# Rank tables prepared earlier, and two small products of a convolution kernel placed one head later

## The chip, the cores and the metric

The kernel runs on one core of a Trainium2 chip. Its time is device microseconds of one execution; a kernel's time is the median over its runs. The core has a matrix engine (TensorE, PE in the profile), VectorE (DVE), ScalarE (ACT), GpSimd (POOL) and SyncE (SP), each with its own instruction stream that it works off in order. They wait for one another by semaphores. SP here does little but issue transfers (SPq in the profile), ACT and POOL issue some too. TensorE reads from on-chip memory and writes to its accumulation memory (PSUM), from where the other engines take the result.

## The reference

Input `x` has 128 sequences of 32 heads of 512 positions. Three things are computed:

```
K  = 2 Re( Ct @ exp(dtA * arange(512)) )           # one 512-tap kernel per head, from log_dt, C, log_A, A_imag
y  = causal_convolution(x, K) + D * x              # per sequence and head
y  = y * (position < length[sequence])             # cut at the sequence's length
g  = sigmoid(y @ gate_w.T) + bias                  # 16 experts; the best 4, weights normalised
o  = sum_e w_e * (silu(y @ Wg_e.T) * (y @ Wu_e.T)) @ Wd_e.T  + the same for one shared expert
out = x + o
```

A row is one sequence and head: 4096 rows of 512. Each goes to four of sixteen experts and to the shared one.

## The kernel before

The kernel has three stages, all bound in large part by TensorE.

**Convolution.** A convolution with a kernel of 512 taps is a product with a Toeplitz matrix. Each head `h` has a strip of 128x512 that holds its taps shifted by one per partition, and `convolve` (L595) multiplies the transposed input of the head by the strip (four products, L611, into a PSUM tile `py`, of which there are three in turn). VectorE multiplies `py` by the length mask (`yb`, L629). Before the change heads 0 and 1 are convolved alone, all later ones in pairs: the main loop (L999) calls `convolve` for a group, and then `behind_head` for each of the group's heads. Pairs leave out work where all sequences are short (a register read from `skips`, and branches on it).

**Where a strip comes from.** The taps are made in six chunks of columns, `CHUNKS = ((0, 2), (2, 2), (4, 2), (6, 4), (10, 4), (14, 2))`, a column being two heads. For each chunk `waves` (VectorE, with ScalarE for the sine and GpSimd for a product) makes powers, and `kernels` forms factors `gg_r`, `gg_i`, `f_r`, `f_i` (VectorE, GpSimd), multiplies them on TensorE (`pk`, L407, small products), adds on VectorE (`krow`, L415), sends `krow` to memory (`kd<-krow`, L422, SP's queue), and `kernel_strip` reads it back with shifted addresses as a strip for four heads (`strip<-kd`, L433, SP's queue, 1 MB in one transfer, for the first strip four of 256 KB). The strip of heads 4 to 7 comes from the second chunk, that of heads 8 to 11 from the third. `waves_at` and `kernels_at` say behind which head each chunk's two parts are called. SP's queue also loads the input of the next four heads (`xt`, L155, 1 MB, issued when the convolution of the last of four heads has freed its buffer).

**Beside it.** `turn_y` transposes each head's result by products with a permutation `to_rank` that sorts sequences by length (`pt`, L635), and ScalarE copies it into `store`. Every four heads `gates` and `sums` give the router's scores (`parts`, L656; `pg`, L673), every eight heads `route` picks experts on VectorE (L695 to L728), and ACT's queue writes `yb` to memory.

**The rank tables.** `ranks` (L512) is a generator: each `next` runs it to its next `yield`. It makes what the later stages need of the sorted order. `by_rank` is a product of `to_rank_h` (a copy of the permutation, L520) and the lengths, L523. `reach` and `reach_sum` come from it, and `k_u` from a product of those, L543. `unit_rows` comes from a product of `same_mod` and `row_u`, L562. Before the change its four parts are called behind heads 24, 25, 26 and 27. `later` and `behind_masks` tie its VectorE instructions behind the masked products issued so far.

**What sets the order.** TensorE's instructions stand in the order in which the program calls them (the manual schedule around the loop). Those of the other engines are placed by a scheduler at build time; ties such as `dep` bind it. Its choice is fixed in the built program.

**Shared expert, then routed experts.** After the convolutions come eight units of shared-expert products (L1072, L1087) among which the routing tables are finished, and then some 134 tiles of routed rows (L1168 to L1226).

Of the kernel before, what the change touches and what calls it, by code (L numbers as in the profile page):

```python
# [28 lines left out]
F32 = mybir.dt.float32  # L29
BF16 = mybir.dt.bfloat16  # L30
F16 = mybir.dt.float16
I32 = mybir.dt.int32
AF = mybir.ActivationFunctionType
ALU = mybir.AluOpType
AX = mybir.AxisListType
# [3 lines left out]
P = 128  # L39
B, H, L, N = 128, 32, 512, 64  # L40
E, TOPK, I = 16, 4, 256
KT = L // P
IT = I // P
HB = 4
# [3 lines left out]
NU = B // UB  # L48
# [8 lines left out]
AHEAD = 4  # L57
NT = (B * H * TOPK - E) // P + E
NT_MIN = B * H * TOPK // P
LAST_DRAIN = NT_MIN - 4  # L60
TS = 64
SKIPS = 4
# [17 lines left out]
def ssm_moe_kernel(  # L80
# [15 lines left out]
    nc = tc.nc  # L96
    WD = 2 * KT * I

    const = ctx.enter_context(tc.tile_pool(name="const", bufs=1))
# [3 lines left out]
    ps_m = ctx.enter_context(tc.tile_pool(name="ps_m", bufs=2, space=PSUM))  # L103
# [54 lines left out]
    def dep(of, on, why):  # L158
        tc.add_manual_dep(of.ins, on.ins.name, SYNC, reason=why)
# [27 lines left out]
    upos = iota("upos", [[-UB, NU]], 0, 1)  # L187
# [93 lines left out]
    CHUNKS = ((0, 2), (2, 2), (4, 2), (6, 4), (10, 4), (14, 2))  # L281
# [182 lines left out]
    def behind_masks(op):  # L464


        dep(op, masks[-1], "later in VectorE's order")
# [14 lines left out]
    for key, raw, own in ((key_row, key_row, cpos), (key_col, len_col, ppos)):  # L482
# [3 lines left out]
        if key is key_col:  # L486
            num_len = const.tile([P, 2], F16, tag="num_len", name="num_len")
# [23 lines left out]

    def ranks():  # L512

        to_rank_h = const.tile([P, P], F16, tag="to_rank_h", name="to_rank_h")
        last_mask = masks[-1]

        def later(op):
            dep(op, last_mask, "later in VectorE's order")

        later(nc.vector.tensor_copy(to_rank_h, to_rank))  # L520

        by_rank_ps = ps_m.tile([P, 2], F32, tag="m", name="by_rank_ps")
        nc.tensor.matmul(by_rank_ps, lhsT=to_rank_h, rhs=num_len, start=True, stop=True)  # L523
        by_rank = const.tile([P, 2], F32, tag="by_rank", name="by_rank")
        behind_masks(nc.vector.tensor_copy(by_rank, by_rank_ps))
        yield


        reach = const.tile([P, KT], BF16, tag="reach", name="reach")
        later(nc.vector.memset(reach, 1.0))  # L530
        for n in range(1, KT):
            nc.vector.tensor_scalar(
                reach[:, n : n + 1], by_rank[:, 1:2], float(n * P), None, ALU.is_gt
            )

        unit = const.tile([P, NU], BF16, tag="unit", name="unit")
        later(nc.vector.tensor_scalar(unit, upos, 0.0, None, ALU.is_equal))
        reach_sum = const.tile([P, 1], F32, tag="reach_sum", name="reach_sum")
        nc.vector.tensor_reduce(reach_sum, reach, AX.X, ALU.add)
        reach_b = const.tile([P, 1], BF16, tag="reach_b", name="reach_b")  # L540
        nc.vector.tensor_copy(reach_b, reach_sum)
        k_u_ps = ps_m.tile([1, NU], F32, tag="m", name="k_u_ps")
        nc.tensor.matmul(k_u_ps, lhsT=reach_b, rhs=unit, start=True, stop=True)  # L543
        yield
        k_u = const.tile([1, NU], I32, tag="k_u", name="k_u")
        behind_masks(nc.vector.tensor_copy(k_u, k_u_ps))


        div = const.tile([P, 2], F32, tag="div", name="div")
        mod = const.tile([P, 1], F32, tag="mod", name="mod")  # L550
        later(floor_div(div[:, 0:1], rank, UB))
        later(floor_div(div[:, 1:2], ppos, UB))
        nc.vector.scalar_tensor_tensor(mod, div[:, 0:1], -float(UB), rank, ALU.mult, ALU.add)
        same_mod = const.tile([P, P], F16, tag="same_mod", name="same_mod")
        nc.vector.tensor_scalar(same_mod, pmod, mod, None, ALU.is_equal)
        row_u = const.tile([P, NU], F16, tag="row_u", name="row_u")
        nc.vector.tensor_scalar(
            row_u, cpos[:, :NU], div[:, 0:1], ppos, ALU.is_equal, ALU.mult
        )
        yield  # L560
        row_ps = ps_m.tile([P, NU], F32, tag="m", name="row_ps")
        nc.tensor.matmul(row_ps, lhsT=same_mod, rhs=row_u, start=True, stop=True)  # L562
        part = const.tile([P, TU // P], F32, tag="part", name="part")
        nc.vector.tensor_scalar(
            part, cpos[:, : TU // P], float(P // UB), div[:, 1:2], ALU.mult, ALU.add
        )
        unit_rows = const.tile([P, NU, TU // P], I32, tag="unit_rows", name="unit_rows")
        rows = nc.vector.scalar_tensor_tensor(
            unit_rows,
            row_ps.unsqueeze(2).to_broadcast([P, NU, TU // P]),  # L570
            float(H),
            part.unsqueeze(1).to_broadcast([P, NU, TU // P]),
            ALU.mult,
            ALU.add,
        )
        behind_masks(rows)
        of_ranks.update(by_rank=by_rank, reach=reach, k_u=k_u, unit_rows=unit_rows)


    skips = const.tile([1, 1], I32, tag="skips", name="skips")  # L580
# [22 lines left out]
    def convolve(tb, qs, xt, yb):  # L603
        heads = [(q, pys[(tb * HB + q) % len(pys)]) for q in qs]

        def products(n):
            c0 = n * TS
            for q, py in heads:
                for jt in range(KT):

                    nc.tensor.matmul(  # L611
                        py[:, c0 : L - jt * P],
                        lhsT=xt[:, jt, q, :],
                        rhs=strip[tb][:, q, jt * P + c0 :],
                        start=(jt == 0),
                        stop=(jt == KT - 1 or L - (jt + 1) * P <= c0),
                    )
                    if L - (jt + 1) * P <= c0:
                        break

        if len(qs) == 1:
            products(0)
        else:

            if not skip:
                skip[0] = nc.tensor.value_load(skips[0:1, 0:1], min_val=0, max_val=SKIPS - 1)
            by_number(skip[0], 0, SKIPS - 1, products)
        for q, py in heads:
            masks.append(nc.vector.tensor_mul(yb[:, q, :L], py, within))  # L629
# [316 lines left out]


    waves_at = dict(zip((0, 1, 4, 9, 15), CHUNKS[1:]))
    kernels_at = dict(zip((0, 3, 8, 14, 20), CHUNKS[1:]))
    weights_at = {19: 0, 27: 1}  # L950
    made_waves, strips, k_us = {}, [1], {}
    ybs, xbs, rest_of_ranks = {}, {0: load_xt(0)}, ranks()
# [2 lines left out]
    def behind_head(h):  # L955

        tb, q = divmod(h, HB)
        if h in waves_at:
            made_waves[waves_at[h]] = waves(*waves_at[h], 0)[0]
        if h in kernels_at:  # L960
            c = kernels_at[h]
            chunk_last[c[0]] = kernels(*c, *made_waves[c])
            behind_masks(chunk_last[c[0]])

        if strips[-1] in (tb, tb + 1) and strips[-1] < NB and strips[-1] * HB in kd_of:
            kernel_strip(strips[-1])
            strips.append(strips[-1] + 1)
        if 24 <= h <= 27:
            next(rest_of_ranks, None)
        if h in weights_at:  # L970
            weights_out(weights_at[h])
        if q == 2 and tb > 0:
            gates(tb - 1)
        last = h == H - 1
        for each in turns_at(h):
            turn_y(each, ybs[each // HB])
        if q == 3 and tb > 0 and not last:
            sums_and_route(tb - 1)
        if last:

            sums_and_route(tb - 1)
            k_us[0] = nc.tensor.value_load(of_ranks["k_u"][0:1, 0:1], min_val=1, max_val=KT)
            turned = turn_y(h, ybs[tb])
            gates(tb)
            return turned
# [10 lines left out]
            route(tb // RB)  # L996

    with tc.manual_schedule(engines={mybir.EngineType.PE}):
        for h, n in [(0, 1), (1, 1), *((h, 2) for h in range(2, H, 2))]:  # L999
            tb, q = divmod(h, HB)  # L1000
            if q == 0:
                ybs[tb] = yp.tile([P, HB, L], F32, tag="yb", name=f"yb{tb}")
                if tb + 1 < NB:
                    xbs[tb + 1] = load_xt(tb + 1)
            convolve(tb, range(q, q + n), xbs[tb], ybs[tb])
            if q + n == HB:
                nc.scalar.dma_start(out=y_bh[:, tb * HB : (tb + 1) * HB, :L], in_=ybs[tb])
            for each in range(h, h + n):
                turned = behind_head(each)
# [5 lines left out]
    by_rank, reach, k_u, unit_rows = (of_ranks[k] for k in ("by_rank", "reach", "k_u", "unit_rows"))  # L1015
# [242 lines left out]
    with tc.manual_schedule(engines=None):  # L1258
# [36 lines left out]
        unit_step(NU)  # L1295
        for step in range(1, NT_MIN + 2):
            if step == LAST_DRAIN:
                nc.gpsimd.drain(fusable=False)
# [12 lines left out]

        rest(NT_MIN + 2)

# [50 lines left out]
```

## Time and profile before

| | us |
|---|---|
| median of 4 runs | 913.96 |
| lowest, highest | 913.42, 916.12 |
| profiled execution, its own time | 913.1 |
| its span | 911.4 |
| TensorE busy in the span | 872.4 (96%) |
| first convolution starts | 23.05 |
| first product of the shared expert starts | 123.11 |

The profiled execution is 1.7 us longer than its span, which runs from the first to the last recorded instruction. Times in the profile are from the span's start. In a line of the timeline come start, duration, engine, line, operation, output and inputs, shape and count; in brackets stands how long the engine was idle before and what ended it. Lines of windows give the busy time of each engine in a stretch, then the TensorE clock that was granted (1.00 is full), the share of the transfer engines' time in use, and GB/s.

### The profile page before, as it was taken

The page shows a single profiled execution, that of the slowest core. Times are in us where ns is not written, and L with a number is a line of the kernel's source. Part 1 is how long each engine was busy: PE and PEld are TensorE (multiplying, and loading weights), DVE is VectorE, ACT ScalarE, POOL GpSimd, SP SyncE. Part 2 cuts the span into 40 slices and gives each one's busy share as a digit, 9 for nine tenths or more (in the row PEclk, how much of TensorE's full clock was granted, in tenths as well). Part 3 has the DMA queues.
Part 4 walks back from the last instruction along what each step waited for, and adds up shares of the span by engine and source line. Part 5 has one row for each costly group of instructions (what it writes and reads, how often), then busy time and mean ns, then how long its engine had stood idle before and what let it go on. Part 6 is the DMA issues. An engine that isn't in the chain of part 4 may idle for free.

```text
span 911.4 us, 14680 instructions
## 1 busy us (share of the span) xinstructions
PE 872.4 (96%) x2976; PEld 444.9 (49%) x2976; DVE 415.0 (46%) x1488; ACT 189.1 (21%) x379; POOL 420.8 (46%) x372
## 2 busy tenths in 40 slices
PE   2999999999999999999999999999999999999994
PEld 1677654444444444445444544454444544454441
DVE  8988564968802334333342334333333323344332
ACT  1222221111221112211221222122221112122221
POOL 2210011422473556645565456545645455566554
PEclk9999999999999999999999999999999999999998
DMA  5788566786697667766677667655755556567565
GB/s 191 222 273 278 188 234 198 197 209 126 125 218 218 122 116 129 159 140 116 119 138 171 116 107 138 117 109 108 142 107 108 111 96 117 107 132 133 109 126 100
DMA packets 54710, 136.03 MB, mean 149 GB/s; under 512 B 12432, under 2 KB 12592, under 8 KB 50992
## 3 DMA queue, kind: packets, MB, share of 16 engines
q0 software_dynamic: 36256, 89.77, 52.3%
q1 hardware_dynamic: 14096, 36.15, 11.8%
q10 hardware_dynamic: 4224, 8.39, 2.5%
q8 instruction: 76, 1.25, 0.5%
q14 instruction: 58, 0.48, 0.2%
HBM read 288.08 MB, written 60.64 MB: 383 GB/s over the span
## 4 chain that ended last, share of the span: by engine, by line
PE 67%; SPq 2%; issue 1%; POOL 0%; DVE 0%; ACT 0%; ACTq 0%
PE g L1200 35%; PE o L1226 24%; PE m L1168 4%; PE u L1218 3%; PE o L1087 1%; SPq L1251 1%; SPq L1305 0%; SPq L1288 0%; SPq L1287 0%; SPq L1286 0%; POOL out L1236 0%; SPq L1023 0%; DVE zt L1212 0%; ACT sgt L1211 0%; SPq L1308 0%
## 5 line engine op out<-in xcount | busy, mean ns | idle before, releaser
L1200 PE MATMUL g<-store,yt 128*128 x742 | 343.0, 596 | 1.8 <-issue 1.3
L1236 POOL DMA_INDIRECT out<-ob,put x134 | 212.2, 1584 | 234.7 <-DVE junk L1175 188.3
L1226 PE MATMUL o<-store,zT 128*128 x536 | 252.1, 592 | 0.0
L1212 DVE SCALAR_TENSOR_TENSOR zt<-g,wt,sgt 128x256 f32<-128x256 f32 x135 | 65.3, 484 | 306.5 <-ACT sgt L1211 302.2
L1200 PEld LDWEIGHTS g<-store,yt 128*128 128x128 f32 x742 | 130.3, 190 | 118.7 <-issue 117.7
L1226 PEld LDWEIGHTS o<-store,zT 128*128 128x128 f32 x536 | 101.4, 190 | 128.8 <-issue 124.1
L1037 POOL DMA_INDIRECT yg<-y_rows,get x140 | 138.4, 989 | 49.4 <-issue 30.4
L1235 DVE COPY ob<-o 128x512 f32<-128x512 f32 x134 | 92.7, 692 | 109.2 <-PE o L1226 105.1
L1174 ACT COPY yt<-m 128x512 f32<-128x512 f32 x136 | 79.7, 586 | 225.9 <-PE m L1168 216.3
L1211 ACT ACTIVATE sgt<-g 128x256 f32<-128x256 f32 x135 | 51.9, 384 | 268.5 <-PE g L1200 224.4
L1096 POOL DMA_INDIRECT out<-ob,unit_rows x32 | 50.2, 1570 | 91.9 <-ACT ob L1094 57.0
L1168 PEld LDWEIGHTS m<-ident,yg 128*128 128x128 f32 x373 | 48.7, 141 | 72.2 <-issue 71.8
L611 PE MATMUL py<-strip,xt 128*128 128x192 f32 (+7 forms) x256 | 63.2, 400 | 0.7 <-DMA strip<-kd 0.7
L1168 PE MATMUL m<-ident,yg 128*128 128x128 f32 x373 | 63.0, 273 | 0.7 <-issue 0.5
L1087 PE MATMUL o<-store,z 128*128 128x512 f32 x128 | 57.6, 596 | 1.1 <-ACT yt L1174 1.1
L1221 DVE COPY zT<-u 128x256 f32<-128x256 f32 x134 | 56.3, 421 | 0.6 <-issue 0.4
L611 PEld LDWEIGHTS py<-strip,xt 128*128 128x128 f32 x256 | 43.9, 193 | 19.4 <-issue 13.8
L1218 PE MATMUL u<-ident,zt 128*128 128x128 f32 x268 | 51.2, 273 | 0.6 <-DVE zt L1212 0.6
L1072 PE MATMUL g<-store 128*128 128x512 f32 x92 | 42.9, 601 | 1.2 <-issue 0.9
L1072 PE MATMUL u<-store 128*128 128x512 f32 x92 | 42.2, 593 | 0.0
L914 DVE TENSOR_SCALAR cols<-tpos_h,stl,tok 128x143 f16<-128x143 f16 x128 | 42.0, 332 | 0.0
L1087 PEld LDWEIGHTS o<-store,z 128*128 128x128 f32 x128 | 23.4, 190 | 26.7 <-issue 25.4
(285 smaller groups left out, 492.6 us busy)
## 6 DMA issues: line engine op xcount, KB each, us to landing
store<-in_w_all SPq DMA_DIRECT2D x143, 1536.0 KB
xt<-in_x_t SPq DMA_DIRECT2D x8, 1024.0 KB
y_rows<-yb ACTq DMA_DIRECT2D x8, 1024.0 KB
out<-in_x POOLq DMA_DIRECT2D x8, 1024.0 KB
strip<-kd SPq DMA_DIRECT2D x7, 1024.0 KB
yg<-y_rows,get POOLq DMA_INDIRECT x140
out<-ob,put POOLq DMA_INDIRECT x134
strip<-kd SPq DMA_DIRECT2D x4, 256.0 KB
```

Of the source, the lines that this page charges most:

```text
L611: nc.tensor.matmul(py[:, c0 : L - jt * P], lhsT=xt[:, jt, q, :], rhs=strip[tb][:, q, jt * P + c0 :], start=(jt == 0), stop=(jt == KT - 1 o ...
L1037: nc.gpsimd.indirect_dma_start(out=at(yg, t), out_offset=None, in_=y_rows[:, :], in_offset=bass.IndirectOffsetOnAxis(ap=made["get"][:, t : ...
L1072: nc.tensor.matmul(ps[it], lhsT=w_sh[:, c0 : c0 + P], rhs=yT[:, u, kt, :, :].rearrange("p h b -> p (h b)"), start=(kt == KT - n), stop=(kt ...
L1087: nc.tensor.matmul(po, lhsT=at(zu, u)[:, it, q * P : (q + 1) * P], rhs=w_sh[:, c0 : c0 + L], start=(it == 0), stop=(it == IT - 1),)
L1168: nc.tensor.transpose(pt[:, q, :], at(yg, t)[:, q * P : (q + 1) * P], ident)
L1174: nc.scalar.copy(at(yt, t), pt)
L1200: mm = nc.tensor.matmul(pgu, lhsT=at(yt, t)[:, q, :], rhs=ring_flat[:, bass.ds(w0s[t] + q * 2 * I, 2 * I)], start=(q == KT - n), stop=(q = ...
L1212: nc.vector.scalar_tensor_tensor(at(zs, t), pgu[:, I:], at(wts, t), sg, ALU.mult, ALU.mult)
L1218: nc.tensor.transpose(at(p_z, t)[:, it, :], at(zs, t)[:, it * P : (it + 1) * P], ident)
L1226: mm = nc.tensor.matmul(po, lhsT=at(zts, t)[:, it, :], rhs=ring_flat[:, bass.ds(w0s[t] + WD + it * L, L)], start=(it == 0), stop=(it == IT ...
L1235: nc.vector.tensor_copy(ob, po)
L1236: add = nc.gpsimd.indirect_dma_start(out=out, out_offset=bass.IndirectOffsetOnAxis(ap=made["put"][:, t : t + 1], axis=0), in_=ob, in_offse ...
```

## The change

Four edits. The preparation in `ranks` that needs no product (`to_rank_h`, `unit`, `div`, `mod`, `same_mod`, `row_u`, `part`) is gathered in its first part; the products `by_rank_ps` and `row_ps` and what hangs on them come in the second part, `k_u_ps` in the third. The parts are called behind heads 22, 25 and 29 in place of 24 to 27. The second chunk's `kernels` is called behind head 1 in place of 0, the third's behind head 4 in place of 3; in `behind_head`, `kernels` now comes ahead of `waves`. Heads 4 and 5 are convolved alone, with what is called behind head 4 between them; like a pair's, their products still leave out work by `skips`.

```diff
+GROUPS = [(0, 1), (1, 1), (2, 2), (4, 1), (5, 1)] + [(h, 2) for h in range(6, H, 2)]
...
     def ranks():
...
         later(nc.vector.tensor_copy(to_rank_h, to_rank))
-
-        by_rank_ps = ps_m.tile([P, 2], F32, tag="m", name="by_rank_ps")
-        nc.tensor.matmul(by_rank_ps, lhsT=to_rank_h, rhs=num_len, start=True, stop=True)
-        by_rank = const.tile([P, 2], F32, tag="by_rank", name="by_rank")
-        behind_masks(nc.vector.tensor_copy(by_rank, by_rank_ps))
-        yield
+        unit = const.tile([P, NU], BF16, tag="unit", name="unit")
+        later(nc.vector.tensor_scalar(unit, upos, 0.0, None, ALU.is_equal))
 
         reach = const.tile([P, KT], BF16, tag="reach", name="reach")
         later(nc.vector.memset(reach, 1.0))
-        for n in range(1, KT):
-            nc.vector.tensor_scalar(
-                reach[:, n : n + 1], by_rank[:, 1:2], float(n * P), None, ALU.is_gt
-            )
-
-        unit = const.tile([P, NU], BF16, tag="unit", name="unit")
-        later(nc.vector.tensor_scalar(unit, upos, 0.0, None, ALU.is_equal))
-        reach_sum = const.tile([P, 1], F32, tag="reach_sum", name="reach_sum")
-        nc.vector.tensor_reduce(reach_sum, reach, AX.X, ALU.add)
-        reach_b = const.tile([P, 1], BF16, tag="reach_b", name="reach_b")
-        nc.vector.tensor_copy(reach_b, reach_sum)
-        k_u_ps = ps_m.tile([1, NU], F32, tag="m", name="k_u_ps")
-        nc.tensor.matmul(k_u_ps, lhsT=reach_b, rhs=unit, start=True, stop=True)
-        yield
-        k_u = const.tile([1, NU], I32, tag="k_u", name="k_u")
-        behind_masks(nc.vector.tensor_copy(k_u, k_u_ps))
...
-        yield
-        row_ps = ps_m.tile([P, NU], F32, tag="m", name="row_ps")
-        nc.tensor.matmul(row_ps, lhsT=same_mod, rhs=row_u, start=True, stop=True)
         part = const.tile([P, TU // P], F32, tag="part", name="part")
...
+        yield
+
+        by_rank_ps = ps_m.tile([P, 2], F32, tag="m", name="by_rank_ps")
+        nc.tensor.matmul(by_rank_ps, lhsT=to_rank_h, rhs=num_len, start=True, stop=True)
+        by_rank = const.tile([P, 2], F32, tag="by_rank", name="by_rank")
+        behind_masks(nc.vector.tensor_copy(by_rank, by_rank_ps))
+        row_ps = ps_m.tile([P, NU], F32, tag="m", name="row_ps")
+        nc.tensor.matmul(row_ps, lhsT=same_mod, rhs=row_u, start=True, stop=True)
...
         behind_masks(rows)
+        for n in range(1, KT):
+            nc.vector.tensor_scalar(
+                reach[:, n : n + 1], by_rank[:, 1:2], float(n * P), None, ALU.is_gt
+            )
+
+        reach_sum = const.tile([P, 1], F32, tag="reach_sum", name="reach_sum")
+        nc.vector.tensor_reduce(reach_sum, reach, AX.X, ALU.add)
+        reach_b = const.tile([P, 1], BF16, tag="reach_b", name="reach_b")
+        nc.vector.tensor_copy(reach_b, reach_sum)
+        yield
+        k_u_ps = ps_m.tile([1, NU], F32, tag="m", name="k_u_ps")
+        nc.tensor.matmul(k_u_ps, lhsT=reach_b, rhs=unit, start=True, stop=True)
+        k_u = const.tile([1, NU], I32, tag="k_u", name="k_u")
+        behind_masks(nc.vector.tensor_copy(k_u, k_u_ps))
...
-        if len(qs) == 1:
+        if tb * HB + qs[0] < 2:
             products(0)
...
-    kernels_at = dict(zip((0, 3, 8, 14, 20), CHUNKS[1:]))
+    kernels_at = dict(zip((1, 4, 8, 14, 20), CHUNKS[1:]))
...
-        if h in waves_at:
-            made_waves[waves_at[h]] = waves(*waves_at[h], 0)[0]
         if h in kernels_at:
             c = kernels_at[h]
             chunk_last[c[0]] = kernels(*c, *made_waves[c])
             behind_masks(chunk_last[c[0]])
+        if h in waves_at:
+            made_waves[waves_at[h]] = waves(*waves_at[h], 0)[0]
...
-        if 24 <= h <= 27:
+        if h in (22, 25, 29):
             next(rest_of_ranks, None)
...
-        for h, n in [(0, 1), (1, 1), *((h, 2) for h in range(2, H, 2))]:
+        for h, n in GROUPS:
```

## The prediction

> **What bounds the kernel now.** I read the page first, then the waits of TensorE, then the timelines of TensorE, SP and VectorE around the two edited places, then windows of half a microsecond for the clock.
>
> ```profile
> span 911.4 us, 14680 instructions
> PE 872.4 (96%) x2976; PEld 444.9 (49%) x2976; DVE 415.0 (46%) x1488; ACT 189.1 (21%) x379; POOL 420.8 (46%) x372
> ```
>
> TensorE is busy for 96% of the span, and behind the convolutions its windows of 20 us are full but for a few waits that it takes with it (1.02 us by 180, 1.07 at 265). So a microsecond won or lost before 123 should reach the end. The first edited place:
>
> ```profile
> 23.05 2.40 PE L611 MATMUL py<-strip,xt 128*128 128x512 f32 x8 [0.40 <-DMA strip<-kd]
> 26.42 0.22 PE L407 MATMUL pk<-f_r,gg_r 128*32 128x32 f32 x2 [0.98 <-DVE gg_r L400]
> 26.82 6.05 PE L611 MATMUL py<-strip,xt 128*128 128x512 f32 x24
> 32.70 0.61 PE L635 MATMUL pt<-to_rank,yb 128*128 128x128 f32 x4
> 34.02 0.25 PE L407 MATMUL pk<-f_r,gg_r 128*32 128x32 f32 x2 [0.71 <-DVE gg_r L400]
> ...
> 34.95 3.79 PE L611 MATMUL py<-strip,xt 128*128 128x448 f32 x16
> ...
> 58.16 3.89 PE L611 MATMUL py<-strip,xt 128*128 128x448 f32 x16 [0.29 <-DMA strip<-kd]
> ```
>
> Between head 0 and heads 4 and 5 (34.95) TensorE stands twice for VectorE's `gg_r`: 0.98 and 0.71 us. At 34.95 it does not wait for the second strip, at 58.16 it does wait for the fourth. When that second strip is sent:
>
> ```profile
> 27.51 0.33 SPq L422 DMA_DIRECT2D kd<-krow  x1
> 28.93 0.39 SPq L433 DMA_DIRECT2D strip<-kd  x1
> ...
> 52.46 0.37 SPq L433 DMA_DIRECT2D strip<-kd  x1
> ```
>
> It follows `kd<-krow` by 1.42 us. That one follows VectorE's `krow`:
>
> ```profile
> 27.27 0.21 DVE L415 TENSOR_TENSOR krow<-pk,dsk 32x64 f32<-32x64 f32 x1
> ```
>
> The second edited place, heads 24 to 27:
>
> ```profile
> 92.86 3.87 PE L611 MATMUL py<-strip,xt 128*128 128x448 f32 x16
> 97.84 0.18 PE L523 MATMUL by_rank_ps<-num_len,to_rank_h 128*128 128x2 f16 x1 [1.12 <-DVE to_rank_h L520]
> ...
> 99.10 0.17 PE L543 MATMUL k_u_ps<-unit,reach_b 128*1 128x8 bf16 x1 [0.59 <-DVE reach_b L541]
> 99.20 1.12 PE L635 MATMUL pt<-to_rank,yb 128*128 128x128 f32 x4
> 100.11 5.02 PE L611 MATMUL py<-strip,xt 128*128 128x448 f32 x16
> 105.06 1.06 PE L656 MATMUL parts<-store,gw 128*32 128x512 f32 x8
> ```
>
> Two waits for VectorE, and behind them a pair that takes 5.02 us where others take 3.8. The windows say why: the granted clock (the number behind the engines) is halved.
>
> ```profile
> 98.50:99.00 0.50, 0.02 (x1) 0.00 (x0) 0.50 (x8) 0.45 (x1) 0.00 (x0) 1.00 1.04 406
> 99.50:100.00 0.50, 0.50 (x4) 0.50 (x3) 0.00 (x0) 0.00 (x0) 0.00 (x0) 0.50 0.80 307
> 102.00:103.00 1.00, 1.00 (x5) 0.70 (x4) 0.00 (x0) 0.00 (x0) 0.00 (x0) 0.71 0.03 10
> ```
>
> From the mixed windows (0.67 in 99.0 to 99.5, 0.71 in the last) the fall runs from 99.17 to 102.58, 3.4 us.
>
> **Rank tables: a gain of 3.6 us.** In the built program TensorE has, behind the pair of heads 24 and 25: turn of 22, `by_rank_ps`, `row_ps`, turn of 23, next pair. Steps between starts elsewhere: a pair 3.72 (39.45 to 43.17), two turns 0.87 (38.58 to 39.45), and the two small products 0.2 (97.84 to 97.88 and the like, with their loads). That is 3.72 + 0.87 + 0.2 + 3.72 = 8.5, say 8.6, where 105.06 - 92.86 = 12.20 stands: 3.6 less. Of these the waits are 1.7, the halved clock 1.7 (half of 3.4), the rest order. VectorE's preparation, about 1.9 us, moves ahead of the mask of head 24, where it had been idle 1.24 us; the masks of 24 and 25 come some 0.6 us later, at 96.3 and 96.9, and head 27, which needs head 24's accumulator back, starts only at 99.8. So it is covered. `k_u_ps` behind head 29 has its inputs ten microseconds early and costs 0.1, the 0.17 us wait ahead of the old `row_ps` pays for that. If an ordinary run of before has no fall of the clock here, the gain is 1.9: the other end.
>
> **Chunk two behind head 1: a loss of 2.0 us.** The waits of 0.98 and 0.71 go: head 1 starts at 23.05 + 2.27 = 25.3, `pk` at 27.6, the pair at 28.0, two turns later TensorE is ready for head 4 at 28.0 + 3.65 + 0.95 = 32.6. What is late next is the strip. `krow` needs `pk`, which is now done at 28.1 and not at 26.9. And in VectorE's built order `krow` no longer stands behind the second instruction of the third chunk's waves, but behind ten more of them (1.48 us by the steps from 27.41 to 28.89), the mask of head 1 (0.61) and one step of the exponential series (0.29): 27.21 + 1.48 + 0.61 + 0.29 = 29.6, done at 29.8, 2.3 us later than before. By the same steps `kd<-krow` goes at 29.85 and the strip at 31.25. From a strip's issue to the product that waits for it the trace has 5.70 us (52.46 to 58.16); above it is bounded by 6.02 (28.93 to 34.95, no wait), below by 4.7, when the windows behind 28.93 have moved 1 MB. I take 5.25, between the 5.70 that had other transfers beside it and the 4.7. Head 4 starts at 36.5 (36.0 to 37.2), after a wait of 3.9 us. From there all of the old way from 34.95 to head 8 (45.91) follows, with the third chunk's `pk` (0.44), which before lay ahead of 34.95: 36.5 - 34.95 + 0.44 = +2.0 (1.5 to 2.7).
>
> What queues behind this: on SP `xt` for heads 8 to 11, issued at 32.0 right behind the strip, and then the third chunk's `kd` and strip. Head 4 ends at 38.3, mask and `krow` at 39.3, `kd` then has up to 1 MB of `xt` ahead of it in the queue (before, it took 3.91 us from 35.03 to 38.94 for this), strip out by 41 to 42 and in by 46 to 47.5. TensorE comes to head 8 at 48 or later. Covered, by 0.5 to 2 us; no cost taken.
>
> **The clock: a loss of 1.7 us.** Waits of 0.98 and 0.71 us left the clock at 1.00 in the windows around them; 1.12 + 0.59 in 2.4 us halved it. One of 3.9 should. One fall costs half of 3.4, 1.7, as the row of heads 26 and 27 has it (a pair and half a turn: 1.68). It can be 0.9, if half of it lies in the wait itself, or 3.4, two falls in a row; I take one.
>
> **Small ones.** In the built order of ScalarE the sine of the fourth chunk now stands behind the copies of heads 4 and 5's turns. Its factors come at about head 8's start + 3.6 to 3.9, its `pk` is due at + 3.72: 0 to 0.3, I take 0.15. The split of heads 4 and 5 adds two branches, which TensorE's sequencer takes ahead of the products: nothing, 0.2 if not.
>
> **Sum**, against the profiled execution's own 913.1: -3.6 + 2.0 + 1.7 + 0.15 = +0.25, so 913.35. The median shown is 0.86 above that execution; with it, 914.2.
>
> [...]
>
> **Rivals.**
>
> 1. Slower: an ordinary run of before does not have the fall at 99. Then the gain is 1.9, and the sum -1.9 + 3.85 = +2.0, 916.0. For it: two gaps of less than 1.2 us are near what does nothing (0.98), and the runs spread over 2.7 us. Against: the one profile that there is has it and is no slower than the runs. It decides if most runs are without it.
> 2. Slower: the third strip is late as well, at head 8. It decides if that strip lands later than 48 to 49.5, which needs its issue at 43, a microsecond behind my latest. Price: a wait of 1 and another fall of 1.7, 914.2 + 2.7 = 916.9. For it: `yb`'s 1 MB to memory is sent at about 35 and shares the transfer engines with `xt`. Against: head 8 itself moves back with each loss.
> 3. Faster: the strip lands sooner. The first one's quarters took 3.4 us from the first issue (19.65) to head 0 (23.05). At that rate head 4 starts at 34.7, the wait is 2.0, the chunk's term +0.2, and with the clock's 1.7 or without: -1.6 or -3.3, 912.4 to 910.6. Against: that was 256 KB, and 4.7 us is what 1 MB took.
> 4. The tables do not get out of the way (TensorE still waits for VectorE behind head 25): nothing gained, +3.85, 917.8. Against: in the built order all of their preparation stands before the mask of head 24.
>
> **How the numbers follow.** Forecast 0.53, rival 1 0.14, rival 2 0.13, rival 3 0.15, rival 4 0.05. Within 0.2% (1.83 us, about what a measurement of this kernel can tell from no change) lies the forecast, with a little more of it beyond the upper bound than of rival 3 inside the lower: faster 0.15, same 0.52, slower 0.33. The forecast's own range is 912.8 to 916.0, from its bounds in part. The range that leaves out 2 in 10 reaches to rival 2's 916.9 above, and to the forecast without a clock fall and a part of rival 3 below, 912.0.
>
> **What would show it.** Right: no wait of `by_rank_ps` and `k_u_ps`, clock 1.00 there, 8.6 us from the pair of 24 to the `parts` behind 27; no wait of `pk` behind head 1; head 4 waiting 3 to 4.5 us for `strip<-kd`, `krow` at 29.6, and a clock of 0.50 within 4 us of it; head 8 at 49 to 50. Wrong: head 4 without a wait of 2 us, a strip in less than 4.5 us, or a wait at head 8.

## The result and the profile after

The changed kernel takes 914.96 us (median of 44 runs, 913.57 to 919.06), the kernel before beside it 914.13 (70 runs, 911.12 to 917.57). The ratio is 1.0015, with a 95% interval of 1.0008 to 1.0022: 1.4 us slower, 0.7 to 2.0. That is a loss that can be told from zero, and it lies inside the 0.2% within which the forecast put it. The profiled execution takes 913.54 us against 913.1. From the page:

```profile
span 911.8 us, 14685 instructions
PE 871.4 (96%) x2976; PEld 444.7 (49%) x2976; DVE 414.1 (45%) x1488; ACT 189.0 (21%) x379; POOL 421.0 (46%) x372
```

Span and busy time hardly moved; what moved lies ahead of 123 us. The timeline of TensorE in the changed kernel, from the second chunk's `pk` to head 12 (head 4 at 37.71, head 8 at 50.88 and head 12 at 63.12 are the first products of a new strip):

```profile
26.91 0.25 PE L409 MATMUL pk<-f_r,gg_r 128*32 128x32 f32 x2
...
27.82 3.88 PE L612 MATMUL py<-strip,xt 128*128 128x448 f32 x16 [0.47 <-issue]
...
37.71 3.69 PE L612 MATMUL py<-strip,xt 128*128 128x448 f32 x8 [5.13 <-DMA strip<-kd]
...
50.88 3.87 PE L612 MATMUL py<-strip,xt 128*128 128x448 f32 x16
...
63.12 3.89 PE L612 MATMUL py<-strip,xt 128*128 128x448 f32 x16 [0.29 <-DMA strip<-kd]
```

The two waits for `gg_r` are gone. In their place stands one of 5.13 us for the second strip. Head 8 starts at 50.88 where it started at 45.91. VectorE and SP's queue say when that strip could be sent:

```profile
29.44 0.21 DVE L417 TENSOR_TENSOR krow<-pk,dsk 32x64 f32<-32x64 f32 x1
```

```profile
29.68 0.33 SPq L424 DMA_DIRECT2D kd<-krow  x1
31.22 0.39 SPq L435 DMA_DIRECT2D strip<-kd  x1
31.73 0.43 SPq L157 DMA_DIRECT2D xt<-in_x_t  x1
...
44.96 0.37 SPq L435 DMA_DIRECT2D strip<-kd  x1
```

From 31.22 to head 4 at 37.71 pass 6.49 us, with the input of heads 8 to 11 sent half a microsecond behind the strip. The windows around head 4 (the number behind the engines' busy times is the granted clock):

```profile
37.00:37.50 0.50, 0.00 (x0) 0.00 (x0) 0.00 (x0) 0.00 (x0) 0.00 (x0) 1.00 1.01 410
37.50:38.00 0.50, 0.29 (x1) 0.29 (x2) 0.00 (x0) 0.00 (x0) 0.00 (x0) 0.65 1.01 426
...
41.00:42.00 1.00, 1.00 (x14) 0.89 (x14) 0.56 (x1) 0.00 (x0) 0.00 (x0) 0.97 0.95 369
```

The clock is halved from 37.65 to 41.06, 3.4 us; such a stretch is called a fall below. From head 4 to head 8 pass 13.17 us. The second edited place, again TensorE:

```profile
97.48 3.87 PE L612 MATMUL py<-strip,xt 128*128 128x448 f32 x16
...
101.63 0.17 PE L548 MATMUL by_rank_ps<-num_len,to_rank_h 128*128 128x2 f16 x1
...
102.16 3.79 PE L612 MATMUL py<-strip,xt 128*128 128x448 f32 x16
105.87 1.07 PE L657 MATMUL parts<-store,gw 128*32 128x512 f32 x8
...
123.48 1.98 PE L1073 MATMUL g<-store 128*128 128x512 f32 x4 [0.33 <-PE parts L657]
```

No wait stands at `by_rank_ps`, the second pair takes 3.79 us again, the granted clock is 1.00 in every window from 97 to 107, and the stretch takes 8.39 us instead of 12.20. The shared expert starts 0.37 us later than before.

### The profile page after: what moved, and what is told of

It reads as the page before. It is cut to its first block, busy times and chain, and to the rows that moved or that the text cites. A ratio compares the mean times of both kernels' runs of the same rounds, so it can differ in the third digit from the quotient of the medians.

```text
span 911.8 us, 14685 instructions
## 1 busy us (share of the span) xinstructions
PE 871.4 (96%) x2976; PEld 444.7 (49%) x2976; DVE 414.1 (45%) x1488; ACT 189.0 (21%) x379; POOL 421.0 (46%) x372
## 3 DMA queue, kind: packets, MB, share of 16 engines
q10 hardware_dynamic: 4224, 8.39, 2.4%
## 4 chain that ended last, share of the span: by engine, by line
PE 67%; SPq 2%; issue 1%; POOL 0%; DVE 0%; ACT 0%
PE g L1201 35%; PE o L1227 24%; PE m L1169 4%; PE u L1219 3%; PE o L1088 1%; SPq L1252 0%; SPq L1306 0%; SPq L1288 0%; SPq L1287 0%; SPq L1289 0%; POOL out L1237 0%; SPq L1024 0%; DVE zt L1213 0%; ACT sgt L1212 0%; SPq L1309 0%
```

## The experiments

Ratios are to the kernel before on the same chip, with 95% intervals; microseconds are worked out from them on 913.9.

| | ratio | us |
|---|---|---|
| the change | 1.0015 [1.0008, 1.0022] | +1.4 |
| rank tables alone | 0.9974 [0.9959, 0.9990] | -2.4 |
| chunks alone | 1.0061 [1.0039, 1.0084] | +5.6 |
| second chunk back behind head 0 | 1.0001 [0.9989, 1.0013] | +0.1 |
| third chunk back behind head 3 | 1.0037 [1.0025, 1.0050] | +3.4 |
| `krow` ahead of the waves | 1.0022 [1.0006, 1.0038] | +2.0 |
| input load behind head 4 | 1.0097 [1.0078, 1.0115] | +8.9 |
| waits for a strip filled | 1.0014 [1.0000, 1.0027] | +1.3 |
| kernel before, its gaps at 97 to 99 filled | 0.9997 [0.9982, 1.0011] | -0.3 |

**Rank tables alone.** The changed kernel with the chunks as they were:

```diff
-GROUPS = [(0, 1), (1, 1), (2, 2), (4, 1), (5, 1)] + [(h, 2) for h in range(6, H, 2)]
+GROUPS = [(0, 1), (1, 1)] + [(h, 2) for h in range(2, H, 2)]
...
-    kernels_at = dict(zip((1, 4, 8, 14, 20), CHUNKS[1:]))
+    kernels_at = dict(zip((0, 3, 8, 14, 20), CHUNKS[1:]))
...
+        if h in waves_at:
+            made_waves[waves_at[h]] = waves(*waves_at[h], 0)[0]
         if h in kernels_at:
...
-        if h in waves_at:
-            made_waves[waves_at[h]] = waves(*waves_at[h], 0)[0]
```

> The rank tables' edit alone; chunks and groups as before. Theory (two terms that nearly cancel, the tables' gain and the second strip's lateness): the step from the pair of heads 24 and 25 to the parts behind head 27 takes 8.4 to 8.7 us, as in the changed kernel (8.39), for 12.20; head 4 starts at 35.0 without a wait for its strip; the time is 2 to 3.6 us under before, ratio 0.9961 to 0.998. Rival (the tables' preparation only shifts the wait to a later place, or an ordinary run of before has no fall of the clock and waits little there): ratio 0.999 to 1.000.

Measured: 910.87 us against 913.88, 0.9974, the fastest kernel of the study, and by the intervals faster than before and than the change. It lies in the theory's range; the rival's begins where the interval ends, at 0.999. Head 4 starts at 35.03 without a wait. Its TensorE timeline:

```profile
97.72 0.17 PE L548 MATMUL by_rank_ps<-num_len,to_rank_h 128*128 128x2 f16 x1
...
101.97 1.06 PE L657 MATMUL parts<-store,gw 128*32 128x512 f32 x8
...
119.57 3.69 PE L1073 MATMUL g<-store 128*128 128x512 f32 x8 [0.33 <-PE parts L657]
```

From its pair of heads 24 and 25 (93.58) to 101.97 are 8.39 us, as in the changed kernel. The gain of this half of the change is there by itself. By the mean granted clock, 0.9950 in its 12 runs and 0.9949 in 57 of before, it is a gain of waits more than of clock.

**Chunks alone.** The kernel before with the other half:

```diff
+GROUPS = [(0, 1), (1, 1), (2, 2), (4, 1), (5, 1)] + [(h, 2) for h in range(6, H, 2)]
...
-        if len(qs) == 1:
+        if tb * HB + qs[0] < 2:
...
-    kernels_at = dict(zip((0, 3, 8, 14, 20), CHUNKS[1:]))
+    kernels_at = dict(zip((1, 4, 8, 14, 20), CHUNKS[1:]))
...
-        if h in waves_at:
-            made_waves[waves_at[h]] = waves(*waves_at[h], 0)[0]
         if h in kernels_at:
...
+        if h in waves_at:
+            made_waves[waves_at[h]] = waves(*waves_at[h], 0)[0]
```

> The chunks' edit alone (second chunk behind head 1, third behind head 4, heads 4 and 5 alone); rank tables as before. Theory: head 4 waits 4 to 5.5 us for its strip, the clock falls to a half behind it, head 8 starts at 49.5 to 51 (before 45.91), the waits at heads 24 and 25 are there again (1.1 and 0.6 us); the time is 4 to 5 us over before, ratio 1.004 to 1.006. Rival (the loss needs both edits, by VectorE's order): ratio 1.000 to 1.002.

Measured: 919.15 us, 1.0061. Its TensorE timeline:

```profile
37.42 3.46 PE L612 MATMUL py<-strip,xt 128*128 128x448 f32 x8 [4.85 <-DMA strip<-kd]
...
63.77 5.57 PE L612 MATMUL py<-strip,xt 128*128 128x448 f32 x16 [1.46 <-DMA strip<-kd]
...
105.37 0.18 PE L524 MATMUL by_rank_ps<-num_len,to_rank_h 128*128 128x2 f16 x1 [1.69 <-DVE to_rank_h L521]
```

The wait at head 4 is that of the changed kernel (the strip went out at 30.89, 6.53 us before). The loss is all of this half's. Here head 12 (63.77) waits as well, and its pair takes 5.57 us, for 3.89 in the kernel before: a second fall of the clock. The waits of the rank tables are there again, of 1.69 and 0.59 us, and this time the pair behind them takes 3.79 us, without a fall. The two halves' ratios multiply to 1.0035, above the change's 1.0015 but within the width of their intervals.

**Second chunk back behind head 0.** The changed kernel, its third chunk still behind head 4:

```diff
-    kernels_at = dict(zip((1, 4, 8, 14, 20), CHUNKS[1:]))
+    kernels_at = dict(zip((0, 4, 8, 14, 20), CHUNKS[1:]))
...
+        if h in waves_at and not h:
+            made_waves[waves_at[h]] = waves(*waves_at[h], 0)[0]
         if h in kernels_at:
...
-        if h in waves_at:
+        if h in waves_at and h:
```

> The changed kernel with the second chunk's products put back behind head 0; the third chunk's stay behind head 4, and heads 4 and 5 stay alone. Theory (the second chunk's move makes the loss): TensorE waits 1 us for gg_r behind head 0 again, the second strip is sent at 29 as before, head 4 waits 0 to 1 us for it and starts at 34 to 34.9, no fall of the clock, head 8 at 45.3 to 46; the time is 2 to 4 us under before, ratio 0.9955 to 0.998. Rival (the third chunk's move or the split of heads 4 and 5 makes the loss): head 8 at 48 or later, ratio 1.000 or more.

Measured: 1.0001. The theory fell, and its rival held. TensorE and SP's queue:

```profile
34.63 2.05 PE L612 MATMUL py<-strip,xt 128*128 128x448 f32 x8 [0.82 <-DMA strip<-kd]
48.45 5.54 PE L612 MATMUL py<-strip,xt 128*128 128x448 f32 x16 [2.14 <-DMA strip<-kd]
```

```profile
37.74 0.33 SPq L424 DMA_DIRECT2D kd<-krow  x1
41.98 0.37 SPq L435 DMA_DIRECT2D strip<-kd  x1
```

Head 4 is at 34.63, three microseconds sooner, but head 8 now waits 2.14 us for the third strip, and its pair takes 5.54 us at a granted clock of 0.50 from 49.18 on (worked out from 0.59 in the window from 49 to 50). Against the rank tables alone (0.9974), which leave the third chunk where it was, this is 0.0027 or 2.5 us more (the intervals just touch). So the third chunk's move, with the split of heads 4 and 5, costs by itself; in the changed kernel it is hidden, because the second chunk's loss has moved head 8 back to 50.88.

**Third chunk back behind head 3.** The other way round, and so heads 4 and 5 as a pair:

```diff
-GROUPS = [(0, 1), (1, 1), (2, 2), (4, 1), (5, 1)] + [(h, 2) for h in range(6, H, 2)]
+GROUPS = [(0, 1), (1, 1)] + [(h, 2) for h in range(2, H, 2)]
...
-    kernels_at = dict(zip((1, 4, 8, 14, 20), CHUNKS[1:]))
+    kernels_at = dict(zip((1, 3, 8, 14, 20), CHUNKS[1:]))
```

> The changed kernel with the third chunk's products put back behind head 3, and heads 4 and 5 a pair again; the second chunk's stay behind head 1. In VectorE's order krow of the second chunk stays where the change put it; in SP's order the input load now comes behind the third chunk's kd, at about 34.5. Theory (the second chunk's late strip alone is enough for the loss, the third's lateness is covered by it): head 4 waits 3.5 to 5 us for its strip, the clock falls, head 8 at 49 to 50.5, ratio 0.9995 to 1.002. Rival (the third chunk's lateness makes the loss): head 8 at 46 to 47.5, ratio 0.996 to 0.998.

```profile
36.86 5.57 PE L612 MATMUL py<-strip,xt 128*128 128x448 f32 x16 [2.32 <-DMA strip<-kd]
...
63.88 5.57 PE L612 MATMUL py<-strip,xt 128*128 128x448 f32 x16 [2.32 <-DMA strip<-kd]
```

Measured: 1.0037. Head 8 comes at 49.60, as expected, with a fall behind head 4 (its pair takes 5.57 us, for 3.79 in the kernel before). But head 4 waits 2.32 us for its strip and not 3.5 to 5, since two waits for the third chunk's factors (0.96 us for `gg_r`, 0.48 for `gg_i`) now stand ahead of it, and the time is above what was expected: at head 12 stands a wait of 2.32 us that neither theory had, with a second fall (5.57 us for 3.89). This strip was issued at 56.12, 7.76 us before the product.

**`krow` ahead of the waves.** The changed kernel; the first two operations of the third chunk's waves are tied behind the second chunk's `krow`:

```diff
-        if c0:
+        if c0 == 4:
+            dep(first_op, chunk_last[2], "later in VectorE's order")
+        elif c0:
             behind(first_op, c0)
```

> The changed kernel, with the third chunk's waves tied behind the second chunk's krow, so that on VectorE only the mask of head 1 stands ahead of krow and not ten wave instructions and a series step as well. Theory (VectorE's order holds the strip back): krow at 27.8 for 29.44, the strip sent at 29.5 for 31.22; head 4's wait falls from 5.1 to 2.5 to 3.5 us; time 1.5 to 2 us under the changed kernel, ratio to before 0.999 to 1.000. Rival (what counts is how long the strip's transfer takes beside the input load sent behind it): head 4 starts no sooner than 37.

```profile
28.75 0.33 SPq L428 DMA_DIRECT2D kd<-krow  x1
31.63 0.39 SPq L439 DMA_DIRECT2D strip<-kd  x1
```

```profile
38.04 3.88 PE L616 MATMUL py<-strip,xt 128*128 128x448 f32 x8 [5.28 <-DMA strip<-kd]
```

Measured: 1.0022. `kd<-krow` goes 0.9 us sooner, but the strip follows it by 2.88 us where it was 1.54, so head 4 comes no sooner: the rival's sign, though the strip itself takes 6.41 us from its issue as in the changed kernel. SP's queue stands there waiting for `kd<-krow` to land, 2.5 us where it is 1.1 in the changed kernel. Why these 8 KB take longer, with the transfer engines hardly in use (a share of 0.16 and less from 29 to 32), was not settled; an earlier `krow` alone does not bring head 4 forward.

**Input load behind head 4.** The changed kernel, with the load of `xt` for heads 8 to 11 held until head 4's masked product:

```diff
-        nc.sync.dma_start(out=t, in_=x_t[tb])
+        load = nc.sync.dma_start(out=t, in_=x_t[tb])
+        if tb == 2:
+            dep(load, masks[4], "behind the second strip")
...
-                if tb + 1 < NB:
+                if tb + 1 < NB and tb != 1:
                     xbs[tb + 1] = load_xt(tb + 1)
             convolve(tb, range(q, q + n), xbs[tb], ybs[tb])
+            if h == 4:
+                xbs[2] = load_xt(2)
```

> The changed kernel, with the input load of heads 8 to 11 tied behind the mask of head 4, so that it is issued at about 40 and not at 31.73, half a microsecond behind the second strip. Theory (the strip was slow, 6.5 us from its issue to head 4, because of the load that queues right behind it): head 4 starts 5.0 to 5.7 us after the strip's issue, its wait falls from 5.1 to 3.6 to 4.3 us; what is won may be lost again at head 8, where the load and the third strip come later. Rival (a strip takes 6 to 6.5 us by itself): head 4 starts 6.2 us or more after the strip's issue, as in the changed kernel.

```profile
36.60 3.43 PE L614 MATMUL py<-strip,xt 128*128 128x448 f32 x8 [3.78 <-DMA strip<-kd]
...
56.64 5.48 PE L614 MATMUL py<-strip,xt 128*128 128x448 f32 x16 [6.98 <-DMA strip<-kd]
```

The strip went out at 31.32: 5.28 us instead of 6.49. So the load right behind it on the queue is what adds 1.2 us. The whole is 1.0097, since the third strip now comes too late for head 8, which waits 6.98 us: it goes out at 47.32, half a microsecond behind another input load.

**Waits for a strip filled.** The changed kernel, with 16 products whose result nobody reads ahead of head 4, and head 5's mask tied behind the third chunk's `krow`:

```diff
+            if h == 4:
+                keep_warm(masks[2], 16)
             convolve(tb, range(q, q + n), xbs[tb], ybs[tb])
+            if h == 5:
+                dep(masks[5], chunk_last[4], "later in VectorE's order")
```

> The changed kernel with 16 products whose result nobody reads ahead of head 4's convolution (they start when head 2's accumulator is free, at about 33.7, and fill 3.5 us of the wait), and head 5's mask tied behind the third chunk's krow as in the changed kernel's order. Theory (of the loss at the start some 1.7 us is the halved clock): the clock stays at 1.00 behind 37.7, head 4 starts when it did (37 to 38) and head 8 at 49 to 49.4 for 50.88; 1 to 1.7 us under the changed kernel, ratio to before 0.9990 to 1.0005. Rival (the clock's fall costs little, since the products there wait for other things): head 8 at 50.5 or later.

```profile
37.80 2.05 PE L612 MATMUL py<-strip,xt 128*128 128x448 f32 x8 [0.35 <-DMA strip<-kd]
...
49.74 3.86 PE L612 MATMUL py<-strip,xt 128*128 128x448 f32 x16 [0.28 <-DMA strip<-kd]
63.14 3.89 PE L612 MATMUL py<-strip,xt 128*128 128x448 f32 x16 [1.45 <-DMA strip<-kd]
...
123.49 2.83 PE L1077 MATMUL g<-store 128*128 128x512 f32 x6 [0.33 <-PE parts L657]
```

The clock stays at 1.00 (windows from 32 to 44), and head 8 comes 11.94 us behind head 4 instead of 13.17, that is 1.23 us, or 1.51 without the 0.28 that head 8 now waits; head 4's own eight products take 2.05 for 3.69. This shows a fall's price up to head 8. End to end it is 1.0014, nothing won, though the expectation had 0.9990 to 1.0005: head 12 waits 1.45 us here, 0.29 in the changed kernel's profile, and 123.49 is 123.48 again. The runs say the same: their mean granted clock is 0.9953 for the changed kernel's 0.9922, some 1.6 falls fewer, and the time has not moved. What one strip's wait gives back, the next one's takes.

**Kernel before, its gaps filled.** Seven unread products in the two gaps at 97 to 99:

```diff
+        if h in (24, 25):
+            keep_warm(masks[22], {24: 5, 25: 2}[h])
         if 24 <= h <= 27:
```

> The kernel before, with 5 and 2 products whose result nobody reads ahead of the rank products behind heads 24 and 25, so that TensorE is busy in the two waits. Theory (of the tables' gain of 3.6 some 1.7 us is the halved clock and the rest the waits): clock at 1.00 from 99 to 103, the pair of heads 26 and 27 takes 3.8 for 5.02, the step from the pair of heads 24 and 25 to the parts behind head 27 takes 10.4 to 10.7 for 12.20; ratio 0.998 to 0.9995, by how many runs of before have the fall. Rival (no ordinary run has the fall): ratio 0.9998 to 1.0003.

```profile
97.50 0.18 PE L523 MATMUL by_rank_ps<-num_len,to_rank_h 128*128 128x2 f16 x1
...
103.06 1.07 PE L656 MATMUL parts<-store,gw 128*32 128x512 f32 x8
```

The step (from 92.51) is 10.55 us, without a fall (the pair of heads 26 and 27 takes 3.79 us), and yet 0.9997 shows no gain; its interval reaches down to 0.9982 (1.6 us), so that one fall in every second run could hide in it. Either the ordinary run of before has no fall there, or the gain is lost behind it. Three more profiles of the kernel before, with no edit, look for the fall.

**Kernel before again, three times.**

> The kernel before as it stands, profiled again: is the fall of the clock at 99 us there in its ordinary runs? The theory of the prediction: yes, two gaps of about 1.1 and 0.6 us in 2.4 us halve it, 12.2 us from the pair of heads 24 and 25 to the parts behind 27, granted clock 0.50 for 3.4 us between 97 and 105. Rival 1: most runs lack it; then 10.4 to 10.6 us and a clock of 1.00 there. The mean granted clock of the runs measured so far speaks for the rival: 0.99488 for 57 runs of the kernel before, 0.99506 for 36 runs of the three kernels whose profiles have no fall; one fall is 0.0019.

> The same again, for how often it falls. Prediction: 12.2 us and a clock of 0.50 in this stretch; rival 1: 10.4 to 10.6 us and 1.00.

> The same a third time. Prediction: 12.2 us and a clock of 0.50 in this stretch; rival 1: 10.4 to 10.6 us and 1.00. A profile without the fall should then have its first shared product at about 121.4 instead of 123.11, unless other waits before it are longer.

TensorE in the first and in the third:

```profile
92.80 3.87 PE L611 MATMUL py<-strip,xt 128*128 128x448 f32 x16
97.79 0.18 PE L523 MATMUL by_rank_ps<-num_len,to_rank_h 128*128 128x2 f16 x1 [1.12 <-DVE to_rank_h L520]
...
99.05 0.17 PE L543 MATMUL k_u_ps<-unit,reach_b 128*1 128x8 bf16 x1 [0.58 <-DVE reach_b L541]
...
103.36 1.06 PE L656 MATMUL parts<-store,gw 128*32 128x512 f32 x8
```

```profile
92.72 3.87 PE L611 MATMUL py<-strip,xt 128*128 128x448 f32 x16
97.71 0.18 PE L523 MATMUL by_rank_ps<-num_len,to_rank_h 128*128 128x2 f16 x1 [1.12 <-DVE to_rank_h L520]
...
98.97 0.17 PE L543 MATMUL k_u_ps<-unit,reach_b 128*1 128x8 bf16 x1 [0.59 <-DVE reach_b L541]
...
104.97 1.06 PE L656 MATMUL parts<-store,gw 128*32 128x512 f32 x8
```

The gaps are the same to 0.01 us, and one has 10.56 us and the other 12.25. The second of the three is like the first (10.55). So of four profiles two have the fall and two have not: the pair of heads 26 and 27 takes 5.02 us (the first profile) and 5.40 (the third repeat), and 3.79 in the other two. The two with it take 913.1 and 912.7 us, the two without 911.8 and 911.9, so of the 1.65 us some 1.0 is still there at the end. The mean granted clock of the timed runs puts it lower: 0.99488 (57 runs, standard error 0.00018) beside 0.99506 (36 runs of the rank tables alone and the two with filled waits, 0.00019), where a fall is 0.0019 (half of 3.4 us in 912). That is 0.1 falls a run, with an uncertainty of 0.14, if those three kernels have none in their timed runs, as in their profiles no pair of heads from head 4 to the shared expert takes more than 3.89 us.

**The changed kernel again.**

> The changed kernel as it stands, profiled again. Its mean granted clock (0.9922 in 46 runs) is 0.0027 below that of the kernel before, about 1.4 falls of 3.4 us. If each run has one fall at head 4 and some have a second, the stretch from head 4 to head 8 is 13.2 us again, and a second fall may stand at head 12 behind a wait of over 1 us, or the first may last 6.8 us. Rival: the first profile was the usual case, one fall and a wait of 0.3 us at head 12.

Measured: 917.59 us. TensorE, and two of the windows:

```profile
37.94 3.64 PE L612 MATMUL py<-strip,xt 128*128 128x448 f32 x8 [5.32 <-DMA strip<-kd]
...
64.85 5.57 PE L612 MATMUL py<-strip,xt 128*128 128x448 f32 x16 [1.75 <-DMA strip<-kd]
```

```profile
37.00:38.00 1.00, 0.07 (x1) 0.07 (x1) 0.00 (x0) 0.00 (x0) 0.00 (x0) 0.88 1.05 416
65.00:66.00 1.00, 1.00 (x2) 0.50 (x3) 1.00 (x5) 0.00 (x0) 0.84 (x3) 0.54 0.97 410
```

The wait and fall at head 4 repeat (13.22 us to head 8). A second fall stands at head 12, behind a wait of 1.75 us for the fourth strip, and the shared expert starts at 126.88 instead of 123.48. The mean granted clock of the changed kernel's 46 runs, 0.9922, is 0.0027 below that of before, 1.4 falls more per run: the one at head 4, and by this a second one in some.

## Why the prediction was right, and where it was not

The time, the likeliest case (within 0.2%) and most steps came out; one term was mis-sized, one wait was not foreseen, and that the sum met the median is in part luck. Against the two profiled executions:

| term | predicted, us | measured, us |
|---|---|---|
| rank tables | -3.6 | -3.81 (8.39 for 12.20) |
| chunk two behind head 1 | +2.0 | +3.20 (37.71 - 34.95 + 0.44) |
| clock fall behind head 4 | +1.7 | +1.77 (13.17 - 10.96 - 0.44) |
| sine of the fourth chunk | +0.15 | 0 (no wait at its `pk`, 54.67) |
| between heads 8 and 24 | 0 | -0.35 |
| from behind head 27 to the shared expert | 0 | -0.44 |
| sum | +0.25 | +0.37 at 123 us, +0.44 in the time |

**Rank tables: right in this execution.** No wait at either product, clock 1.00, 8.39 us for 8.6. But the fall that makes up 1.7 of the 3.6 is in two of four profiles, so the gain of a run is 2.2 or 3.8 (10.56 or 12.20, less 8.39), as the lower end of this step said. The rank tables alone, at -2.4 [-3.7, -0.9], allow both. The masks of heads 24 and 25 start 3.00 and 3.91 us behind their pair, for 2.87 and 3.90 before, and not 0.6 later as expected.

**Chunk two: the steps right, the strip's transfer mis-sized.** TensorE was ready for head 4 at 32.58 (predicted 32.6), `krow` started at 29.44 (29.6), `kd<-krow` went at 29.68 (29.85) and the strip at 31.22 (31.25). The term that failed is the time from a strip's issue to its product: taken as 5.25 us between 4.7 and 5.70, bounded by 6.02, measured 6.49. So the wait was 5.13 and not 3.9, and head 4 at 37.71 fell out of 36.0 to 37.2. The text had named the cause, "`xt` for heads 8 to 11, issued at 32.0 right behind the strip", and counted it against the third chunk's transfers only, not against the strip that it follows. The time from issue to a product that waits for it, against the distance of the next load on SP's queue:

| kernel, strip | next load behind it, us | issue to product, us |
|---|---|---|
| the change, second | 0.51 | 6.49 |
| chunks alone, second | 0.83 | 6.53 |
| second chunk back, third | 1.54 | 6.47 |
| third chunk back, second | 3.46 | 5.45 |
| second chunk back, second | 3.97 | 5.64 |
| input load behind head 4, second | 9.47 | 5.28 |

The last line is the same kernel with the load moved, so the 1.2 us are shown to be the load's. It is not a law for all strips: the fourth strip, with a load 2.0 to 2.7 us behind it, took 5.5 to 7.8 us in different kernels, and why is open. The third strip of that last kernel, with a load 0.45 us ahead of it, took 9.32.

**Head 8's cover: held, for another reason than given.** The third strip went out at 44.96 and not by 42, because the second chunk's loss was longer. It still was in time, because head 8 itself came at 50.88 and not at 49 to 50. With head 8 at 49.74 (waits filled) it waited 0.28, with head 8 ready at 46.3 (second chunk back) 2.14. This is what the text had against rival 2, and it decided: that rival's point, an issue at 43, was passed by 2 us without its wait.

**The clock: right in this execution.** One fall of 3.4 us that costs 1.77 up to head 8; the second profile has two. End to end the price shows in the spread of the runs: a straight line of time against granted clock gives 1.7 us (standard error 0.2) for a fall's 0.0019 through the 57 runs of before, and 1.9 (0.25) through the changed kernel's 46.

**Small ones.** The sine cost nothing. Ahead of the pair of heads 2 and 3 stood 0.47 us in which TensorE waited for nothing that the profile shows; the wait at head 4 took it up.

**Why the sum held.** The strip's missing 1.2 us were met by four small terms the other way: 0.2 at the tables, 0.15 at the sine, 0.35 ahead of head 24 (it is in the step from 91.03 to 97.48, 6.45 for 6.78; not traced further), 0.44 behind head 27 (of it 0.41 are the waits of 0.17 at `row_ps` and 0.24 at a turn, both gone). The closeness of the sum is better than its parts.

**Not foreseen: head 12.** No step looked at the fourth strip. In the second profile of the changed kernel it costs a wait of 1.75 and a fall, in the first 0.29 and none.

**Rivals.** Rival 1's condition is met in half of the profiles and in more of the runs by their clock; its 916.0 and the forecast's 914.2 lie on both sides of the measured 914.96. With the tables' gain at 3.8 the measured terms sum to +0.4, at 2.2 to +2.0, and the change's +1.4 lies between. But that is with one fall more. By the clock the changed kernel's runs have 1.4 more than those of before: at 1.77 each they cost 2.5, the other terms with the tables at 2.2 come to +0.2, and +2.7 is twice what was measured. So the forecast met the median in part by luck. Rival 3 fell with the 6.49 us. Rival 4 fell: no wait behind head 25. What stays open is the account of the medians: before's four profiled executions (913.1, 911.8, 911.9, 912.7; the last three on another chip than the timed runs of the experiments) all lie under its median of 914.13, and no profile shows what its ordinary runs lose more.

## What to carry to other kernels

When a transfer becomes the last thing waited for, price it with whatever its queue sends right behind it (here 6.49 us from issue to product, and 5.28 with the load moved away), not by an earlier transfer behind which that queue was quiet for longer. An edit's halves want separate runs: here one gains 2.4 us and the other gives back more, and the first alone is the better kernel. A wait of one or two microseconds on the matrix engine cost here itself plus, in some executions only, 3.4 us at half the clock behind it (the same gaps of 1.12 and 0.59 us in two of four); price it as a chance, and look at several profiles before counting that fall as gain or loss.

## What the runs showed of the hardware

A 1 MB load issued 0.5 to 1.5 us behind another 1 MB transfer on the same queue delayed the first one's arrival from 5.3 to 5.6 us to 6.4 to 6.5 (issue to product; second and third strips, the fourth does not follow it).

The same pair of gaps (1.12 and 0.59 us) halved TensorE's granted clock in two of four profiles of one kernel. Waits of 1.75, 1.82, 2.14 and 2.32 us did so where they stood (the pairs behind them take 5.54 to 5.57 us, others 3.79 to 3.89); one of 1.46 did at head 12 of the chunks alone (its pair takes 5.57 us), one of 1.45 at the same place with the waits filled did not (3.89), nor did 1.69 and 0.59 us at the rank tables of the chunks alone (3.79). What decides it was not shown.

Where the windows of a profile show a fall from its start to its end, it lasted 3.4 us, in seven cases of six profiles: 99.17 to 102.58 in the kernel before and 99.47 to 102.88 in its third repeat, 37.65 to 41.06 in the changed kernel, 37.76 to 41.18 and 65.08 to 68.48 in its second profile, 36.88 to 40.28 in the chunks alone, 49.18 to 52.60 with the second chunk back (worked out from the windows with a clock between 0.50 and 1.00). Behind the 5.28 us wait of `krow` ahead of the waves more was lost: from head 4 to head 5 pass 4.99 us, for 2.84 with the waits filled. Those 2.15 us, if all from a clock of 0.50, would be 4.3 us of it: by this estimate more than a fall of 3.4. Its profiled execution and that of the input load behind head 4 (waits of 3.78 and 6.98 us) have a mean granted clock of 0.989, where those of the changed kernel's second profile, of the chunks alone and of the third chunk back, with two falls, have 0.992, 0.993 and 0.993.
